# Transformer block on one core: normed rows stored from ScalarE's queue, tokens reordered within a block, h tiles rotated

## The chip, the cores and the metric

The kernel runs on one core of a Trainium2 chip. The time is that of one execution on the device, in microseconds (us). Before the change it is 1671.27 us, the median of 3 runs (1671.19 to 1672.89). All profile views come from one profiled execution.

A core has five engines that run side by side, each in the order of its own instructions: TensorE (PE, the matmuls; its weight loads are shown as PEld), VectorE (DVE), ScalarE (ACT), GpSimd (POOL) and SyncE (SP). SyncE issues most of the transfers. Transfers themselves are carried by 16 DMA engines. In a view, `SPq` and `ACTq` stand for the queue side of SyncE and ScalarE, `L903` for line 903 of the kernel.

## The reference

One block of a transformer over 2048 tokens of 1024 channels, in float32: attention with one head of 256 channels, then a feed-forward layer of 2752 hidden channels. Each half is a layer norm, the layer, another layer norm, and the residual.

```python
q, k, v = split(layernorm(x) @ Wqkv + bqkv)            # 2048 x 256 each
a  = softmax(q @ k.T / 16) @ v @ Wo + bo
x1 = x + layernorm(a)
xn = layernorm(x1)
h  = silu(xn @ W_gate.T) * (xn @ W_up.T)               # 2048 x 2752
out = x1 + layernorm(h @ W_down.T)
```

(This is the reference with its reshapes left out. The norms have no learned scale.)

## The kernel before

**Precision.** Each float32 operand of a matmul is split into a high part (a cast by ScalarE, L111) and a low part (a subtraction by VectorE, L112). Three matmuls of 128x128 weights against 128x512 then make one product (`mm3`, `mmc`, L867). The splits are most of what VectorE and ScalarE do.

**Stages.** (1) Up to about 200 us: q, k and v. (2) To about 480 us: the attention loop, 16 steps `i` of 128 query tokens, a "block". Step `i` turns the softmaxed scores of block `i` (`turn`), forms the scores of block `i + 1` (`scores`, `softmax`), multiplies by v (`attend`) and projects block `i - 1` (`turn_o`, L478, and `proj`). (3) To about 890 us: `gate_up` for the first 1024 tokens (`s = 0`), ten pairs of hidden blocks at about 40 us each. (4) To about 1042 us: `run_down` for the same tokens, which ends with `finish` for eight blocks. (5) To about 1440 us: `gate_up` for the other 1024 tokens (`s = 1`). (6) `run_down` for these, and the end.

**The feed-forward layer as seven products.** Both `gate_up` and `run_down` treat their matrices as 2 x 2 blocks and form seven products in place of eight. `gate_up` makes seven h matrices per pair (A11, A12, A22, S1, S2, S3, S4), each 128x512, in eight tiles `tmp[0..7]` under the names g11, u11, g12, u12, g22, u22 and g21 (the eighth is not used). Each is stored to DRAM (`put`, L898) and read back by `run_down`. The first products of a pair are copied from PSUM into g11 and u11 (the copy into u11 is L903). The last four stores of a pair are S1 from u22, S3 from u12, S2 from u11 and S4 from g12.

**From rows to columns.** The norm before the feed-forward layer gives rows (a token per partition), while the products want columns (a channel per partition). For a block `t`, `residual` forms x1, stores it to `x1_d[t]`, and leaves the normed rows in a tile `a` (L510, ScalarE). `regroup` stores these rows to `xn_d[t]` in a different order (L597, on SyncE) and reads the result back into tile `b` (L598, on SyncE, once L597 has landed). `xpose` transposes `b` in 32x32 squares on VectorE (L602, output with a stride of 4 elements) and stores the columns to `xT_d` (L604, SyncE). Blocks 0 to 7 (`EARLY = 8`) take this path in steps 2 to 10 of the attention loop: `residual` and `regroup` in step `t + 2`, `xpose` one step later. Blocks 8 to 15 take it during `gate_up` for `s = 0`, one block a pair. There the jobs of a pair (`jobs`) are called at fixed points between its products: the first does nothing, the second (`ahead`) transposes the block of the pair before and loads the next into `f4[2]` and `f4[3]`, the third (`behind`) calls `residual` and `regroup`.

**The end of a block.** `finish` normalises `y`, adds x1 and stores the block to `out` in two halves of 256 KB (L1105; the last block of all in one half and two quarters). For `s = 0` it reads x1 at L1094 into one of two ring tiles, `wr[1]` and `bo_s` (`raws2`), writes the result there or into `y` (L1104), stores it, and frees the tile. For `s = 1` the eight x1 tiles are loaded by L1343 once the room of the columns is free; the halves of that stage's stores alternate between SyncE and ScalarE.

**Order.** Each engine runs its instructions in a fixed order, which a list scheduler works out ahead of time from estimated durations; instructions given to `pin` keep the order in which the program names them. Waits between engines are semaphores. A tile is written again only when its last reader is done, a store's landing included.

Of the kernel before, what the change touches and what calls it, by code (L numbers as in the profile page):

```python
# [34 lines left out]
def block_kernel(ctx, tc, x, xt, wqk, wqk_t, wv, bqk, bv, wo, bo, wgu, wlast, wd, out):  # L35
# [556 lines left out]
        pin(nc.vector.tensor_tensor(wo_s[:, d, 1, :], wr[d], f32(wo_s[:, d, 0, :]), ALU.subtract))  # L592


    def regroup(t, a, b):

        nc.sync.dma_start(xn_d[t].rearrange("(i s) (g c) -> i s g c", i=4, g=4).rearrange("i s g c -> (s g) i c"), a.rearrange("p (i c) -> p i c", i=4))  # L597
        nc.sync.dma_start(b, xn_d[t])  # L598

    def xpose(t, a, b):  # L600

        nc.vector.transpose(a.rearrange("p (j s g) -> p g j s", j=8, g=4), b.rearrange("p (g j c) -> p g j c", g=4, j=8))  # L602
        d = xT_d[t // TB][:, (t % TB) * P : (t % TB + 1) * P]
        nc.sync.dma_start(d.rearrange("(j p) t -> p j t", p=P), a.rearrange("p (j t) -> p j t", j=8))  # L604

    def two(t):
        return t.rearrange("p (j n) -> p j n", j=2)
# [278 lines left out]
    def gate_up(s, p, wg, wu, bg, jobs, behind=None):  # L886


        ag, au, cg, cu = bg
        g11, u11, g12, u12, g22, u22, g21 = tmp[0:7]  # L890
        job = list(jobs)

        def background():
            if job:
                job.pop(0)()

        def put(name, t):
            nc.sync.dma_start(hd[s][p][name], t)  # L898

        prod(ag, wg, "A11", "B11")  # L900
        nc.scalar.copy(g11, ag)
        prod(au, wu, "A11", "B11")
        nc.scalar.copy(u11, au)  # L903
        background()
        prod(cg, wg, "A12", "B21")
        wg.slot[0].done()
        add(g11, cg, g11)
        silu(g11, g11)
        prod(cu, wu, "A12", "B21")
        wu.slot[0].done()  # L910
        add(u11, cu, u11)
        add(g11, g11, u11, ALU.mult)
        put("A11", g11)
        background()
        prod(ag, wg, "S2", "T2", False, behind and behind[0])
        nc.scalar.copy(g12, ag)
        with tc.issue_after(behind[1]) if behind else nullcontext():
            prod(au, wu, "S2", "T2", False)
        nc.scalar.copy(u12, au)
        with tc.issue_after(behind[1]) if behind else nullcontext():  # L920
            prod(cg, wg, "S1", "T1")
        wg.slot[1].done()
        with tc.issue_after(behind[1]) if behind else nullcontext():
            prod(cu, wu, "S1", "T1")
        wu.slot[1].done()
        background()
        prod(ag, wg, "S3", "T3", False)
        nc.scalar.copy(g22, ag)  # L928
        add(g22, cg, g22)
        silu(g22, g22)  # L930
        prod(au, wu, "S3", "T3", False)
        nc.scalar.copy(u22, au)
        add(u22, cu, u22)
        add(g22, g22, u22, ALU.mult)
        put("A22", g22)
        background()
        prod(ag, wg, "A22", "T4", False)
        wg.slot[3].done()
        silu(g21, ag)
        prod(au, wu, "A22", "T4", False)  # L940
        wu.slot[3].done()
        add(g21, au, g21, ALU.mult)
        put("A12", g21)
        prod(cg, wg, "S4", "B22", False)
        wg.slot[2].done()
        add(g12, cg, g12)
        silu(g12, g12)
        prod(cu, wu, "S4", "B22", False)
        wu.slot[2].done()
        add(u12, cu, u12)  # L950
        add(g12, g12, u12, ALU.mult)
        add(u22, g12, g22)
        add(u12, g11, g12, ALU.subtract)
        add(u11, u22, g11, ALU.subtract)
        add(g12, g21, u11, ALU.subtract)
        put("S1", u22)
        put("S3", u12)
        put("S2", u11)
        put("S4", g12)
# [126 lines left out]
    def finish(t, s, yt, spare=None, kept=False, parted=False):  # L1086


        if parted:
            st_, s = s, s[:, 12:32]  # L1090
            nc.vector.bn_aggr(s[:, 12:14], st_[:, 0:24])
        xt_ = raws2.get() if spare is None else spare
        if spare is None:
            nc.sync.dma_start(xt_, x1_d[t])  # L1094
        if not parted:
            nc.vector.bn_aggr(s[:, 12:14], s[:, 0:12])
        nc.vector.tensor_scalar(s[:, 14:15], s[:, 13:14], EPS, None, ALU.add)
        nc.gpsimd.tensor_tensor(s[:, 15:16], s[:, 14:15], mhalf, ALU.pow)
        nc.vector.tensor_scalar(s[:, 16:17], s[:, 12:13], -1.0, None, ALU.mult)
        nc.scalar.activation(yt[:, R], yt[:, R], AF.Identity, bias=s[:, 16:17])  # L1100
        nc.vector.tensor_scalar(yt[:, L], yt[:, L], s[:, 12:13], None, ALU.subtract)
        o = yt if kept else xt_
        for i, h in enumerate((L, slice(512, 768), slice(768, 1024)) if parted else (L, R)):
            nc.vector.scalar_tensor_tensor(o[:, h], yt[:, h], s[:, 15:16], xt_[:, h], ALU.mult, ALU.add)  # L1104
            (nc.sync if spare is None or i % 2 == 0 else nc.scalar).dma_start(out[t * P : (t + 1) * P, h], o[:, h])  # L1105
        if spare is None:
            raws2.free(xt_)

# [93 lines left out]
    for i in range(NT):  # L1202
        more = i + 1 < NT
        if i % TB == 0 and TB <= i < NT - TB:
            q_load(i // TB + 1)
        turn(i, 0)
        turn(i, 1)
        if i == NT - 1:
            for f in order[:2]:
                f.use()  # L1210
            for f, r in zip(order[4:6], f4[2:4]):
                f.load(r)
        if more:
            scores(i + 1, 0)
            scores(i + 1, 1)
        turn(i, 2)
        turn(i, 3)
        if more:
            scores(i + 1, 2)
            scores(i + 1, 3)  # L1220
            softmax(i + 1)

        if i < 2:
            wo_split(i)
        if i == 1:
            q_load(1)
        if i == 2:
            q_split(1, pin)
        if i % TB == 0 and TB <= i < NT - TB:
            q_split(i // TB + 1, pin)  # L1230
        if 2 <= i < EARLY + 2:
            residual(i - 2, *pair[(i - 2) % 3], sts[i - 2], pin)
            regroup(i - 2, *pair[(i - 2) % 3])
        if i < 3:
            nc.sync.dma_start(pair[i][1], x[i * P : (i + 1) * P, :])
        if i == NT - 1:
            for f in order[2:5]:
                f.use()
            for f, r in zip(order[6:8], (wr[1], f4[1])):
                f.load(r)  # L1240
        if i > 0:
            turn_o(i - 1)
        attend(i)
        if i > 0:
            proj(i - 1)
        if 3 <= i < EARLY + 3:
            xpose(i - 3, *pair[i % 3])
        if 3 <= i < EARLY:
            nc.sync.dma_start(pair[i % 3][1], x[i * P : (i + 1) * P, :])
        if 0 < i <= EARLY:  # L1250
            sts[i - 1] = out_stats(i - 1, pair[(i - 1) % 3][0])
        cb = i - EARLY - 3
        if 0 <= cb < 4:
            first_sums(cb, *room[cb % 2])
        if 0 <= cb + 1 < 4:
            first_load(cb + 1, *room[(cb + 1) % 2])
        if i == NT - 4:
            feed.pump()
        if i == NT - 2:
            for n in range(2):  # L1260
                slots.free(flat(a2[:, 2 * n : 2 * n + 2, :, :]))
            feed.pump()
            order = [t2[0], t13[0], t13[1], t13[2], t2[1], t13[3]] + t4
            spare = f4[2], f4[3], wr[1], xe
            for f, r in zip(order, spare):
                f.load(r)
# [17 lines left out]
    def late(p):  # L1284
        return EARLY + p - 1 if 1 <= p <= NT - EARLY else None

    def ahead(p):
        if p == 0:
            with tc.issue_after(last_o[0].ins):
# [3 lines left out]
                        order[9].load(f4[3])  # L1293
            return
        if late(p - 1):
            xpose(late(p - 1), *f4[2:4])
        if late(p):
            nc.sync.dma_start(f4[2], at_d[late(p)])
            nc.sync.dma_start(f4[3], x[late(p) * P : (late(p) + 1) * P, :])
        down_weights(p - 1)  # L1300

    def behind(p):
# [5 lines left out]
        with tc.issue_after(pairs[1][0].loading.ins) if p == 0 else nullcontext():  # L1308
            load_down(p)
        if late(p):  # L1310
            residual(late(p), *f4[2:4])
            regroup(late(p), *f4[2:4])

    for s in range(2):
        pairs, rest, dn = half[s]
        bg, other = (X, Y) if s == 0 else (Y, X)
        for p in range(NPAIR):
            jobs = [] if s else [lambda: None, lambda: ahead(p), lambda: behind(p)]
            if s == 0 and p == 0:
                jobs = [lambda: None, lambda: ahead(0), lambda: behind(0)]  # L1320
            if s == 0 and p == NPAIR - 1:
                jobs.append(lambda: down_weights(NPAIR - 1))
            gate_up(s, p, *pairs[p], bg, jobs, (turned.ins, projected.ins) if s == 0 and p == 0 else None)
# [15 lines left out]
        else:  # L1339
            xpool.release()  # L1340
            x1pool = pool("x1", side="right")
            x1 = [tl(x1pool, [P, C], F32, f"x1_{k}") for k in range(2 * TB)]
            run_down(s, dn, other, bg, x1, [lambda k=k: nc.sync.dma_start(x1[k], x1_d[2 * TB + k]) for k in range(2 * TB)])  # L1343
    xipool.release()
    wpool.release()
    v_pool.release()
# [40 lines left out]
```

## Time and profile before

| what | value |
|---|---|
| median of 3 runs | 1671.27 us |
| the profiled execution | 1671.44 us |
| its span, first to last instruction | 1669.7 us |
| granted TensorE clock, mean | 0.997 |
| DMA moved | 300.38 MB, mean 180 GB/s |

Where the transfers that the change touches stand (median time from issue to landing):

| transfer | issued by | count, size | us to landing |
|---|---|---|---|
| x1 stored, `x_d<-f` | SyncE | 14 x 512 KB | 2.6 |
| normed rows stored, `xn_d<-f` | SyncE | 14 x 512 KB | 3.7 |
| normed rows read, `f<-xn_d` | SyncE | 14 x 512 KB | 5.1 |
| x1 read, first half, `wr<-x_d` and `bo_s<-x_d` | SyncE | 4 + 4 x 512 KB | 5.2 and 4.5 |
| x1 read, second half, `x<-x_d` | SyncE | 8 x 512 KB | 7.8 |
| out stored, `out<-x` | SyncE, ScalarE | 8 + 7 x 256 KB | 2.1 and 2.0 |

The span is the time from the first to the last instruction of the profiled execution; the remaining 1.7 us of its time lie outside. In the views that follow, a line of a timeline gives the start, the length, the engine, the line of the kernel, the operation, the output and inputs by the program's names, the number of instructions merged into the line, and in brackets how long the engine had been idle before it and what it waited for. The chain of waits is followed back from the last instruction: each piece is what released the one after it. `x_d` in these names is `x1_d` of the code; `p_s` and `xi` hold the h tiles.

### The profile page before, as it was taken

How to read it: one execution, taken by the hardware profiler on the slowest of the kernel's cores; microseconds unless marked ns; L12 is line 12 of the kernel's file. 1: busy time of each engine (PE TensorE's matmuls, PEld its weight loads, DVE VectorE, ACT ScalarE, POOL GpSimd, SP SyncE). 2: the span in 40 equal slices, each digit the busy share in tenths (PEclk: the TensorE clock that was granted, in tenths of full speed). 3: DMA queues.
4: the chain of work that ended last, by engine and by line, in shares of the span. 5: the costliest groups of instructions: out<-in, count | busy, mean ns of one | idle time of the engine just before them, and what ended most of it. 6: DMA issues, size and time to landing. Idle time of an engine off the chain costs nothing.

```text
span 1669.7 us, 20815 instructions
## 1 busy us (share of the span) xinstructions
PE 1640.0 (98%) x7576; PEld 1361.9 (82%) x7576; DVE 1133.6 (68%) x1676; ACT 718.5 (43%) x1061; POOL 110.5 (7%) x157
## 2 busy tenths in 40 slices
PE   9999999999999999999999999999999999999998
PEld 8888888788887787877888888788888888888887
DVE  6656778778777777777588457965555665465458
ACT  5663545436443333433365444433333333354342
POOL 3120010000011111111000001100000000000001
PEclk9999999999999999999999999999999999999999
DMA  8451245555656666666568656533222223676653
GB/s 316 166 183 58 66 162 164 180 179 207 228 173 225 226 231 231 226 234 221 192 224 273 196 184 222 191 117 127 104 95 95 96 95 126 222 264 192 201 183 123
DMA packets 148183, 300.38 MB, mean 180 GB/s; under 512 B 14576, under 2 KB 39792, under 8 KB 148080
## 3 DMA queue, kind: packets, MB, share of 16 engines
q1 hardware_dynamic: 146928, 297.08, 52.6%
q10 hardware_dynamic: 1152, 1.97, 0.3%
q8 instruction: 59, 0.97, 0.2%
q14 instruction: 44, 0.36, 0.1%
HBM read 206.70 MB, written 92.29 MB: 179 GB/s over the span
## 4 chain that ended last, share of the span: by engine, by line
PE 73%; DVE 11%; DMA 9%; issue 3%; ACT 1%; POOL 1%; SPq 1%; DVEq 0%; POOLq 0%; ACTq 0%
PE bank L867 56%; PE bank L128 3%; PE bank L130 3%; PE bank L129 3%; DVE a L112 2%; DMA f<-xn_d 2%; PE bank L468 2%; DMA td_T<-f 2%; DVE p_s L881 2%; PE bank L246 1%; DVE small L118 1%; DVE wvo L112 1%; PE bank L452 1%; PE bank L469 1%; DVE f L602 1%
## 5 line engine op out<-in xcount | busy, mean ns | idle before, releaser
L867 PE MATMUL bank<-a 128*128 128x512 f32 (+1 forms) x960 | 226.4, 386 | 0.0
L867 PE MATMUL bank<-xb,a 128*128 128x512 f32 x912 | 212.4, 389 | 1.3 <-DVE a L112 1.3
L867 PEld LDWEIGHTS bank<-a 128*128 128x128 f32 x960 | 179.0, 188 | 36.6
L867 PEld LDWEIGHTS bank<-xb,a 128*128 128x128 f32 x912 | 170.9, 188 | 37.0 <-DVE a L112 1.7
L111 ACT CAST a<-f2p 128x1024 fp32r<-128x1024 f32 (+2 forms) x123 | 107.0, 870 | 127.9 <-PE bank L867 87.8
L112 DVE TENSOR_TENSOR a<-f2p,a 128x1024 fp32r<-128x1024 f32 (+2 forms) x123 | 122.4, 995 | 47.1 <-ACT a L111 43.1
L867 PE MATMUL bank<-kx,a 128*128 128x512 f32 x612 | 147.7, 390 | 0.0
L867 PEld LDWEIGHTS bank<-kx,a 128*128 128x128 f32 x612 | 115.3, 188 | 24.1
L112 DVE TENSOR_TENSOR a<-f,a 128x1024 fp32r<-128x1024 f32 (+1 forms) x70 | 79.9, 1142 | 61.6 <-ACT a L111 59.5
L867 PE MATMUL bank<-wvo 128*128 128x512 f32 (+1 forms) x498 | 120.9, 386 | 0.0
L881 DVE TENSOR_TENSOR p_s<-bank,p_s 128x512 f32<-128x512 f32 x96 | 65.1, 681 | 79.7 <-ACT p_s L903 52.0
L867 PEld LDWEIGHTS bank<-wvo 128*128 128x128 f32 x498 | 92.9, 188 | 18.9
L867 PE MATMUL bank<-kx,wvo 128*128 128x512 f32 x420 | 100.1, 389 | 0.0
L867 PE MATMUL bank<-a,a 128*128 128x512 f32 x420 | 99.6, 389 | 0.3 <-ACT xi L928 0.3
L111 ACT CAST a<-f 128x1024 fp32r<-128x1024 f32 (+1 forms) x70 | 57.5, 822 | 90.2 <-PE bank L867 88.8
L867 PEld LDWEIGHTS bank<-a,a 128*128 128x128 f32 x420 | 78.7, 188 | 17.1 <-ACT xi L928 0.7
L867 PEld LDWEIGHTS bank<-kx,wvo 128*128 128x128 f32 x420 | 78.8, 188 | 16.4
L112 DVE TENSOR_TENSOR wvo<-f,wvo 128x1024 fp32r<-128x1024 f32 (+1 forms) x47 | 54.7, 1163 | 50.9 <-ACT wvo L111 50.9
L867 PE MATMUL bank<-a1b,wvo 128*128 128x512 f32 x360 | 87.2, 390 | 1.5 <-DVE xi L881 1.4
L867 PEld LDWEIGHTS bank<-a1b,wvo 128*128 128x128 f32 x360 | 67.3, 188 | 16.8 <-DVE xi L881 2.8
L867 PE MATMUL bank<-kx 128*128 128x512 f32 (+1 forms) x339 | 78.5, 387 | 0.0
L867 PEld LDWEIGHTS bank<-kx 128*128 128x128 f32 x339 | 63.4, 188 | 13.0
(326 smaller groups left out, 3067.9 us busy)
## 6 DMA issues: line engine op xcount, KB each, us to landing
f2p<-wgu SPq DMA_DIRECT2D x41, 512.0 KB, 5.1
hd_S<-p_s SPq DMA_DIRECT2D x60, 256.0 KB, 4.8
f<-x SPq DMA_DIRECT2D x28, 512.0 KB, 5.6
f<-wgu SPq DMA_DIRECT2D x22, 512.0 KB, 3.5
wr<-wgu SPq DMA_DIRECT2D x21, 512.0 KB, 5.2
f<-wd SPq DMA_DIRECT2D x20, 512.0 KB, 4.2
hd_A<-xi SPq DMA_DIRECT2D x40, 256.0 KB, 2.0
td_T<-f SPq DMA_DIRECT2D x40, 256.0 KB, 4.9
```

The source lines that it names most:

```text
L111: nc.scalar.copy(hi, src)
L112: (lo_engine or nc.vector).tensor_tensor(lo, src, f32(hi), ALU.subtract)
L118: b = nc.vector.bn_stats(s[:, 6 * i : 6 * i + 6], h)
L128: pin(nc.tensor.matmul(o, w[0], m[0], start=first, stop=False))
L129: pin(nc.tensor.matmul(o, w[0], m[1], start=False, stop=False))
L130: return pin(nc.tensor.matmul(o, w[1], m[0], start=False, stop=last))
L246: pin(nc.tensor.matmul(b, xg[:, c, 0, cols], wv_s[:, c, :, :].rearrange("p a f -> p (a f)"), start=(c == 0), stop=False))
L452: nc.tensor.transpose(b[:, n * P : (n + 1) * P], p_s[:, k * P : (k + 1) * P], ident)
L468: nc.tensor.matmul(b, p[:, k, 0, :], vt(k).rearrange("p h d -> p (h d)"), start=(k == 0), stop=False)
L469: nc.tensor.matmul(b[:, D:], p[:, k, 1, :], vt(k, 0), start=False, stop=(k == NKB - 1))
L867: one = nc.tensor.matmul(o, w[i], m[j], start=first and n == 0, stop=last and n == 2, skip_group_check=chained)
L881: nc.vector.tensor_tensor(o, a, b, op)
```

## The change

- `regroup` becomes two functions. `spread` stores the normed rows from ScalarE's queue. `gather` reads them back on SyncE: in the attention loop at the start of the next step, in `gate_up` as the first job of the next pair (`between`).
- `xpose` writes its tile with contiguous output, and the transpose is pinned on VectorE. With it the tokens of a block come out in another order: token `4 s + g` of a block stands at place `32 g + s`.
- To undo that order, x1 is read and `out` is written through `turned_rows`: on the DRAM side 4 groups of 32 rows, with a stride of four rows within a group. It applies to the 8 reads of L1094, the 8 of L1343, and all 33 stores of L1105. The store of x1 keeps its order.
- The names of the h tiles rotate from pair to pair: the next g11 takes the unused tile, the next u11 the tile that held g22.
- `rooms`: in `gate_up` the two tiles of a late block, `f4[2]` and `f4[3]`, swap roles from pair to pair.

```diff
-    def regroup(t, a, b):
-
-        nc.sync.dma_start(xn_d[t].rearrange("(i s) (g c) -> i s g c", i=4, g=4).rearrange("i s g c -> (s g) i c"), a.rearrange("p (i c) -> p i c", i=4))
+    def spread(t, a):
+
+        nc.scalar.dma_start(xn_d[t].rearrange("(i s) (g c) -> i s g c", i=4, g=4).rearrange("i s g c -> (s g) i c"), a.rearrange("p (i c) -> p i c", i=4))
+
+    def gather(t, b):
         nc.sync.dma_start(b, xn_d[t])
 
     def xpose(t, a, b):
 
-        nc.vector.transpose(a.rearrange("p (j s g) -> p g j s", j=8, g=4), b.rearrange("p (g j c) -> p g j c", g=4, j=8))
+        pin(nc.vector.transpose(a.rearrange("p (j g s) -> p j g s", j=8, g=4), b.rearrange("p (g j c) -> p j g c", g=4, j=8)))
...
+    def turned_rows(d):
+        return d.rearrange("(s g) c -> g s c", g=4)
...
         g11, u11, g12, u12, g22, u22, g21 = tmp[0:7]
+        tmp[:] = [tmp[7], g22, g11, g21, u22, u12, u11, g12]
...
-            nc.sync.dma_start(xt_, x1_d[t])
+            nc.sync.dma_start(xt_, turned_rows(x1_d[t]))
...
-            (nc.sync if spare is None or i % 2 == 0 else nc.scalar).dma_start(out[t * P : (t + 1) * P, h], o[:, h])
+            (nc.sync if spare is None or i % 2 == 0 else nc.scalar).dma_start(turned_rows(out[t * P : (t + 1) * P, h]), o[:, h])
...
+        if 3 <= i < EARLY + 3:
+            gather(i - 3, pair[i % 3][1])
...
-            regroup(i - 2, *pair[(i - 2) % 3])
+            spread(i - 2, pair[(i - 2) % 3][0])
...
+    def rooms(p):
+        return f4[2 + p % 2], f4[3 - p % 2]
+
...
         if late(p - 1):
-            xpose(late(p - 1), *f4[2:4])
+            a, b = rooms(p - 1)
+            xpose(late(p - 1), a, b)
         if late(p):
-            nc.sync.dma_start(f4[2], at_d[late(p)])
-            nc.sync.dma_start(f4[3], x[late(p) * P : (late(p) + 1) * P, :])
+            a, b = rooms(p)
+            nc.sync.dma_start(a, at_d[late(p)])
+            nc.sync.dma_start(b, x[late(p) * P : (late(p) + 1) * P, :])
...
         if late(p):
-            residual(late(p), *f4[2:4])
-            regroup(late(p), *f4[2:4])
+            a, b = rooms(p)
+            residual(late(p), a, b)
+            spread(late(p), a)
+
+    def between(p):
+        if late(p - 1):
+            gather(late(p - 1), rooms(p - 1)[1])
...
-            jobs = [] if s else [lambda: None, lambda: ahead(p), lambda: behind(p)]
-            if s == 0 and p == 0:
-                jobs = [lambda: None, lambda: ahead(0), lambda: behind(0)]
+            jobs = [] if s else [lambda: between(p), lambda: ahead(p), lambda: behind(p)]
...
-            run_down(s, dn, other, bg, x1, [lambda k=k: nc.sync.dma_start(x1[k], x1_d[2 * TB + k]) for k in range(2 * TB)])
+            run_down(s, dn, other, bg, x1, [lambda k=k: nc.sync.dma_start(x1[k], turned_rows(x1_d[2 * TB + k])) for k in range(2 * TB)])
```

## The prediction

> **What bounds the kernel now.** I read the page's shares first, then TensorE's timeline for its waits, then the chain of waits and SyncE's timeline at the three places where the edited transfers stand.
>
> ```profile
> PE 1640.0 (98%) x7576; PEld 1361.9 (82%) x7576; DVE 1133.6 (68%) x1676; ACT 718.5 (43%) x1061; POOL 110.5 (7%) x157
> q1 hardware_dynamic: 146928, 297.08, 52.6%
> ```
>
> TensorE is the bound: 1640.0 of 1669.7 us. Only about 30 us are idle, so no edit off TensorE can win more than these plus lost clock, while any edit that starves it adds in full. The queue's line prices a DMA engine: 297.08 MB / (0.526 x 16 x 1669.7 us) = 21.1 GB/s. Where are the idle microseconds that the change can reach? TensorE's timeline, 500 to 800, with the windows around its longest wait (columns: stretch, length, busy of PE, PEld, DVE, ACT, POOL, clock, DMA share, GB/s):
>
> ```profile
> 533.60 1.66 PE L867 MATMUL bank<-qa,a 128*128 128x512 f32 x6 [2.23 <-ACT p_s L903]
> 574.15 1.65 PE L867 MATMUL bank<-qa,a 128*128 128x512 f32 x6 [2.17 <-ACT p_s L903]
> 655.96 2.93 PE L867 MATMUL bank<-qa,a 128*128 128x512 f32 x6 [3.01 <-ACT p_s L903]
> ```
>
> ```profile
> 650.00:660.00 10.00, 6.99 (x24) 5.27 (x23) 3.02 (x6) 1.70 (x3) 0.00 (x0) 0.76 0.94 319
> 660.00:670.00 10.00, 10.00 (x41) 8.19 (x40) 8.59 (x10) 3.53 (x5) 0.00 (x0) 0.90 0.72 230
> 670.00:680.00 10.00, 10.00 (x46) 8.26 (x44) 8.71 (x16) 4.71 (x8) 2.45 (x3) 1.00 0.49 170
> ```
>
> Once a pair TensorE waits for L903, the copy into u11. ACT in turn waits there, up to 5.43 us, for hd_S<-p_s: the store of the last pair's S2 still reads that tile. Six waits sum to 11.5 us. The longest costs more than itself: the clock falls to 0.76, and 650 to 670 holds 65 matmuls where two full windows hold 92; 27 fewer at 0.217 us are 5.9, of which 3.0 is the wait and 2.9 the clock.
>
> Next, the chain of waits where the first half's rows are finished, and the end of the kernel:
>
> ```profile
> 1026.81 4.53 DMA out<-wr
> 1031.41 3.79 DMA wr<-x_d
> 1036.06 0.76 DVE wr L1104
> 1037.26 4.46 DMA bo_s<-x_d
> ...
> 1046.83 1.41 DVE f L1104 x2
> 1048.23 1.15 DVE a L112
> 1049.42 461.79 PE bank L867 x2036
> ```
>
> ```profile
> 1644.61 22.52 SPq L1105 DMA_DIRECT2D out<-x  x9
> ```
>
> Before 1049 the set of output stores, then x1 reloads, through two ring tiles (wr, bo_s) is itself on the chain; behind it TensorE runs unbroken for 462 us. The last nine SyncE stores leave from 1644.61 on, while TensorE works until 1662.9.
>
> **Part 1: the h tiles rotate.** u11 takes the tile that held g22, whose store A22 left in the middle of the last pair. This removes the 11.5 us on L903 and, at the one deep wait, 2.9 of clock: -14.4 at best. The next wait behind is DVE's xi L881 and ACT's xi L928 (0.92, 0.47, 0.30); these 1.7 us stay. I take -14.
>
> **Part 2: stores of normed rows to ACT's queue, reload a step later.** 16 stores leave SyncE at 0.38 us of issue each (526.09, L597), 6 us in sum, and the 16 reloads no longer make it wait for a landing (xn_d<-f: 3.7 us). ACT takes 16 issues at the 0.34 us its own stores show, 5.4 us; each stands right behind L510, an ACT instruction, so it waits only for its engine's own result; behind it stand the L111 casts and u11's copy, 0.34 us late. ACT is 43% busy and idle 1.68 to 5.43 us at a time there: nothing on the path. Without that cover it is 0.34 x 8 = 2.7 us in gate_up. The reload keeps its place on SyncE, after the puts of S1, S3, S2 and S4, and now finds its rows landed; what DVE waits before L602 (19.4 us in 10) mostly goes, on an engine that is not the bound.
>
> **Part 3: the pinned transposes.** The strided L602 takes 2.03 us, 16 times. With contiguous output none is shown: below, the 1.21 us of a 128x1024 tensor_tensor (L506); above, 2.03. In attention it now has a fixed place, behind L491 and ahead of the next L118, L265, L440, L441 and L481. DVE is idle there 1.13 and 1.63 us a step (before L112 at 238.90 and L491 at 250.80), so at most 2.03 - 1.1, about 1 us, reaches TensorE: +8 over 8 steps. Against it TensorE's waits of that stretch, 4.6 (200 to 300) and 1.3, can go: -5.9. The value nearest to both ends is 0, range -5.9 to +8. In gate_up DVE has room (229 of 300 us busy).
>
> **Part 4: reordered rows.** So that the transposes can write contiguously, tokens change places inside a block, and every read of x1_d and store to out now has a DRAM pattern of 4 x 32 rows, row stride 16 KB, where all DMAs of before begin with a count of 64 or 128. 16 reads of 512 KB and 33 stores (31 of 256 KB, 2 of 128) do this. No row shows such a pattern. From below: as today. A 256 KB out<-x lands in 2.0 us and a 512 KB x_d<-f in 2.6, so 256 KB more on 16 engines cost 0.6 us, and about 1.3 is fixed. Above: the transfer is shared by its outermost count, 4 engines of 16, and its engine time is four times as long: 512 KB / (4 x 21.1 GB/s) = 6.2 us, or by the difference of the two landings, 4 x 2 x 0.6 = 4.8. I take T = 5.5 per 512 KB (half for 256), the upper end: equal shares of 4 are what the pattern offers, and no row has a smaller count to show otherwise.
>
> The Trainium skill, "DMA: Bandwidth & Descriptors", states this rule (its rules for kernel authors, and how many engines a transfer uses): an outermost dimension below 16 confines the whole DMA to that many engines. By it the sum is the slower one below, without it the faster one; the trace has no row on either side, and the page speaks against the change.
>
> What T does, place by place:
> - *Finishing the first half.* From 1025.63 to the last x1 reload SyncE issues 12 half stores and 6 reloads, 12 T, and 4 ordinary 512 KB loads at 1.5, each behind the other on the same engines, with wr and bo_s handed from store to reload. 1025.6 + 66 + 6 + 1.3 = 1098.9, where L1104 used it at 1066.57: +32.3. TensorE had some 2.5 us of slack (ACT L919 at 1069.16, needed at 1072.2): +30. DVE works in order, so the stall holds the splits (L112) behind it and TensorE. T = 4.8: +21; 6.2: +38.
> - *The eight x1 loads of the second half.* Issued from 1440.52, 8 T = 44; behind them on SyncE and the engines stand run_down's weights (L848, L849), wanted for the eighth step at 1472.97 (steps are 12 matmuls, 2.72 us, the first at 1453.9). Two 256 KB loads 1.5, landing 1.3, split 2.5: 1440.5 + 49.3 = 1489.8, some 1491 with the small stores between: +18. T = 4.8: +12; 6.2: +24.
> - *The tail.* 8 blocks of out, 8 T, from 1644.6: 1688.6 + 1.3, and about 1 of issue, 1691 against 1669.7: +21. T = 4.8: +16; 6.2: +27.
> - Stalls this long lower the clock as at 650 (2.9 us for one): +4 for the lot, 3 to 5.
>
> **Sum.** Own time 1671.44 (span 1669.7 and 1.7 around it; the median is 1671.27, within 0.2). -14 + 0 + 30 + 18 + 21 + 4 = +59: 1730. With T = 4.8 and the attention gain 1671 - 14 - 6 + 21 + 12 + 16 + 3 = 1703; with T = 6.2 and its loss 1671 - 14 + 8 + 38 + 24 + 27 + 5 = 1759.
>
> **Rivals.** (A) The turned transfers spread as today's do. Then only parts 1 to 3 count: 1671 - 14, 1657, from 1651 to 1665. For it: same bytes, same 4 KB rows. Against: 4 outer entries. (B) The same, and a new wait eats the gain: the pinned transpose costs its +8 and u11's wait only moves, to the spare tile that g11 now takes or to SyncE's later puts, giving back 4 to 7 of the 14: 1668 to 1672, no change. For it: SyncE issues those puts only at 526 to 530, just ahead of the copy. (C) Slower without part 4: the transposes hold DVE in order whenever their reload is late. They do so above 0.9 us a transpose (16 x 0.9 = 14): at the 1.9 us that DVE waits for f<-xn_d today (19.4 / 10), 16 x 1.9 - 14 = +16, 1687. Against it: the reload no longer follows its store.
>
> **Chances.** Forecast 0.82, A 0.12, B 0.04, C 0.02. Range 1690 to 1760: the forecast's bounds, 1703 and 1759, let down most of the way to C, as the low T rests on two landings alone; A and B, 0.16, are left out. What can be told from no change is about 0.2%, 3.3 us: faster 0.12 (A), within it 0.04 (B), slower 0.84.
>
> **What would show it.** Right: x_d reads landing in 7 us or more alone and 256 KB stores in 4 or more; DVE idle before the finishing of rows by DMA; TensorE waits in 1045 to 1100 and near 1475; stores ending some 20 us after TensorE; no waits on u11's copy. Wrong: reads of x1 landing in 4 to 5 us as now (then A); DVE idle before the transposes of 1 us or more (C); a contiguous transpose above 2.03 us, or TensorE waits at L478 that stay (part 3).

## The result, and the profile after

The changed kernel takes 1738.57 us (median of 4 runs, 1736.52 to 1740.45), the kernel before 1671.23 (4 runs). The ratio is 1.0401, 95% interval 1.0383 to 1.0419: 67 us slower. The profiled execution has a span of 1736.3 us.

The first two lines of the page of the changed kernel, engines and the first queue:

```profile
PE 1652.9 (95%) x7576; PEld 1370.7 (79%) x7576; DVE 1122.6 (65%) x1676; ACT 717.9 (41%) x1061; POOL 108.4 (6%) x157
...
q1 hardware_dynamic: 137988, 288.69, 50.1%
```

The bytes are the same, so are the instruction counts of every engine, and VectorE and ScalarE are busy a little less. (Lines stand up to six further down in this kernel: L872 is L867 of the kernel before, L853 is L848, L1110 is L1104 and L1111 is L1105.) TensorE's idle time grew from 30 to 83 us, and its own work is longer by 13 us, with a mean granted clock of 0.974 in place of 0.997. Where? Both kernels issue the same 7576 matmuls, in an order that differs, by the operands' names, in 588 places, most of them between 200 and 320 us. So I set the start of the n-th matmul in the one profile against that in the other. The shift between them changes by more than 0.3 us at these places only (us, negative is earlier; attention is taken to end at 417 us of the kernel before, where its last matmul stands, not at 480):

| stretch | changed against before |
|---|---|
| attention | -6.7 |
| `gate_up`, first half | -18.1 |
| `run_down`, first half, at the first two x1 reads | +7.1 |
| finishing the first half | +40.1 |
| the eight x1 loads of the second half | +22.4 |
| behind TensorE's last matmul | +22.0 |
| sum, with -0.2 ahead of attention (spans 1736.3 and 1669.7) | +66.6 |

Lost time stands at the reordered transfers. The chain of waits of the changed kernel at two of these places (start, length, what):

```profile
1008.86 9.10 DMA out<-wr
1018.03 10.58 DMA wr<-x_d
1029.48 0.76 DVE wr L1110
1030.25 8.46 DMA out<-wr
1038.77 10.32 DMA wr<-x_d
...
1055.25 15.88 DMA wr<-x_d
...
1081.09 11.78 DMA wr<-wgu
...
1487.10 9.17 SPq L853
1496.32 17.25 DMA f2p<-hd_A
```

Before, the same steps were 4.53 for out<-wr and 3.79 for wr<-x_d. The loads of weights and of h that stand behind them (wr<-wgu, f2p<-hd_A) are late with them. TensorE's timeline says the same; its longest wait at each place:

```profile
889.59 0.79 PE L872 MATMUL bank<-a 128*128 128x512 f32 x1 [3.10 <-ACT a L111]
...
1036.95 1.22 PE L872 MATMUL bank<-xb,a 128*128 128x512 f32 x2 [9.04 <-ACT a L111]
...
1502.44 0.79 PE L872 MATMUL bank<-wvo 128*128 128x512 f32 x1 [15.30 <-ACT wvo L111]
```

The releaser named is ScalarE's cast, but the cast had itself waited for a load; at 1036.95 it did so by way of VectorE, which had stood 14.41 us at L1110 for wr<-x_d. The clearest view is the end. SyncE's stores, and the windows behind TensorE's last matmul (columns as in the prediction: the last three are the clock, the share of the 16 DMA engines and GB/s):

```profile
1689.16 30.48 SPq L1111 DMA_DIRECT2D out<-x  x9
```

```profile
1710.00:1720.00 10.00, 0.00 (x0) 0.00 (x0) 2.93 (x8) 0.72 (x1) 0.78 (x1) 0.58 0.26 102
1720.00:1735.00 15.00, 0.00 (x0) 0.00 (x0) 0.00 (x0) 0.00 (x0) 0.00 (x0) 0.50 0.25 94
```

No engine computes any more, only stores run, and they keep 0.25 of the DMA engines' time busy, what 4 of 16 give. At 94 to 102 GB/s a full 512 KB takes 5.1 to 5.6 us.

### The profile page after: what moved, and what is told of

It is laid out like the page before. It is cut to its first block, busy times and chain, and to the rows that moved or that the text cites. A ratio compares the mean times of both kernels' runs of the same rounds, so it can differ in the third digit from the quotient of the medians.

```text
span 1736.3 us, 20865 instructions
## 1 busy us (share of the span) xinstructions
PE 1652.9 (95%) x7576; PEld 1370.7 (79%) x7576; DVE 1122.6 (65%) x1676; ACT 717.9 (41%) x1061; POOL 108.4 (6%) x157
## 4 chain that ended last, share of the span: by engine, by line
PE 77%; DMA 9%; DVE 6%; SPq 2%; issue 2%; ACT 1%; POOL 1%; ACTq 0%; DVEq 0%; POOLq 0%
PE bank L872 56%; PE bank L128 4%; PE bank L130 4%; PE bank L129 4%; PE bank L468 3%; DMA wr<-x_d 2%; DVE a L112 2%; PE bank L469 1%; PE bank L452 1%; DMA xn_d<-f 1%; PE bank L246 1%; DMA out<-wr 1%; SPq L1359 1%; DMA f2p<-hd_S 1%; DMA f2p<-hd_A 1%
## 5 line engine op out<-in xcount | busy, mean ns | idle before, releaser
L872 PE MATMUL bank<-a 128*128 128x512 f32 (+1 forms) x960 | 229.7, 390 | 3.6 <-ACT a L111 3.1
L872 PE MATMUL bank<-xb,a 128*128 128x512 f32 x912 | 217.6, 396 | 15.3 <-ACT a L111 9.0
L872 PEld LDWEIGHTS bank<-xb,a 128*128 128x128 f32 x912 | 173.9, 191 | 53.2 <-ACT a L111 9.5
L872 PEld LDWEIGHTS bank<-a 128*128 128x128 f32 x960 | 180.5, 189 | 41.9 <-ACT a L111 3.5
L872 PE MATMUL bank<-kx,a 128*128 128x512 f32 x612 | 145.1, 389 | 0.0
L872 PE MATMUL bank<-wvo 128*128 128x512 f32 (+1 forms) x498 | 123.1, 391 | 16.0 <-ACT wvo L111 15.3
L872 PEld LDWEIGHTS bank<-kx,a 128*128 128x128 f32 x612 | 115.0, 188 | 24.0
L872 PEld LDWEIGHTS bank<-wvo 128*128 128x128 f32 x498 | 94.3, 191 | 36.2 <-ACT wvo L111 15.7
L872 PE MATMUL bank<-kx,wvo 128*128 128x512 f32 x420 | 101.4, 394 | 0.0
L872 PE MATMUL bank<-a,a 128*128 128x512 f32 x420 | 99.7, 390 | 0.6 <-ACT p_s L934 0.6
L872 PEld LDWEIGHTS bank<-kx,wvo 128*128 128x128 f32 x420 | 80.1, 191 | 16.9
L872 PE MATMUL bank<-a1b,wvo 128*128 128x512 f32 x360 | 88.1, 394 | 5.1 <-DVE xi L886 5.1
L872 PEld LDWEIGHTS bank<-a,a 128*128 128x128 f32 x420 | 78.7, 188 | 17.6 <-ACT p_s L934 1.0
L886 DVE TENSOR_TENSOR xi<-bank,xi 128x512 f32<-128x512 f32 (+1 forms) x90 | 61.0, 682 | 47.4 <-PE bank L872 40.5
L872 PEld LDWEIGHTS bank<-a1b,wvo 128*128 128x128 f32 x360 | 68.7, 191 | 19.9 <-DVE xi L886 5.6
L872 PE MATMUL bank<-kx 128*128 128x512 f32 (+1 forms) x339 | 80.7, 394 | 2.0 <-ACT kx L111 1.2
L886 DVE TENSOR_TENSOR p_s<-bank,p_s 128x512 f32<-128x512 f32 x80 | 53.9, 682 | 43.8 <-PE bank L872 39.9
```

The source lines that it names most:

```text
L872: one = nc.tensor.matmul(o, w[i], m[j], start=first and n == 0, stop=last and n == 2, skip_group_check=chained)
L886: nc.vector.tensor_tensor(o, a, b, op)
```

## The experiments

**What makes the reordered transfers slow.** Three causes fit so far: the outermost count (4), the row stride (16 KB), or a fixed cost of the pattern. Four kernels tell them apart; beside them the kernel before took 1672.37 us.

`plain_rows` takes the reordering out:

```diff
     def turned_rows(d):
-        return d.rearrange("(s g) c -> g s c", g=4)
+        return d
```

> The changed kernel with x1 read and out written without the reordering (so x1 is added to the wrong tokens of a block, and out stands in the reordered order). If all that was lost lies in the reordered transfers, as the prediction says, only its parts 1 to 3 are left: by TensorE's shifts between the two profiles 6.9 us gained in attention and 18.1 in gate_up, so 1671 - 25 = 1646, 1643 to 1650. If something else of the change costs too (pinned transposes, ScalarE's stores, a new order on SyncE), some of the 67 us stay: above 1655.

Measured: 1646.76 us, ratio 0.9854 (0.9839 to 0.9869). All four losses are gone (0.0, +0.2, 0.0, 0.0 in the order of the table), attention keeps -6.8 and `gate_up` -15.3. Everything that was lost lies in the reordered transfers. It is lost in two ways, as TensorE's idle time and as its clock. This is its line here, for the same matmuls as in the changed kernel:

```profile
PE 1634.6 (99%) x7576; PEld 1360.6 (83%) x7576; DVE 1120.6 (68%) x1676; ACT 717.0 (44%) x1061; POOL 110.2 (7%) x157
```

Against it TensorE's own work in the changed kernel is 18.3 us longer (1652.9), at a mean granted clock of 0.974 in place of 0.999, and its idle time 70.4 us longer (83.4 and 13.0). `gate_up` gains 2.8 less than in the changed kernel, in two waits of 0.72 and 1.29 us for the copy into g22 and in clock. The order of instructions on each engine there, by line and tile, is the same in both. The profiled execution is the longest of its four (1649.42, the others 1645.74 to 1647.53), so 2.8 us may be this one execution's; in the profiles of `groups_2` and `groups_16`, with the same order, `gate_up` gains 13.7 and 17.4. A difference of 3 or 4 us in `gate_up` between two profiles means little.

`groups_2` and `groups_16` change the count, `g=4` to `g=2` and `g=16`, and with it the row stride, to 8 and 64 KB.

> The changed kernel with 2 groups of 64 rows (row stride 8 KB) in place of 4 of 32 (16 KB) in every read of x1 and store of out; the order of tokens is then not the right one. By the outermost count: 2 engines, T doubles from 5.5 to about 11 us per 512 KB; 12 T in the finishing of the first half, 8 T at the x1 loads, 8 T in the tail, some 2 T at the first two reads: +30 x 5.5 = +165, about 1900, 1850 to 1950. By the row stride (rows far apart are slow): a smaller stride, so no more than 1739. By a fixed cost of the less simple pattern: the same as 4 groups, 1739.

Measured: 1887.02 us, one run. The same end in its windows:

```profile
1840.00:1860.00 20.00, 0.00 (x0) 0.00 (x0) 4.34 (x11) 1.44 (x2) 0.78 (x1) 0.50 0.13 51
```

0.13 is the share of 2 engines of 16, and the bytes per second are half. Place by place the loss grows from 7.1, 40.1, 22.4 and 22.0 us to 13.6, 100.5, 60.9 and 61.2. With 12, 8 and 8 times T on the path of the last three, doubling T added 60.4 / 12, 38.5 / 8 and 39.2 / 8: by this growth T on 4 engines is 4.8 to 5.0 us, a little under the 5.1 to 5.6 of the rates above.

> The same with 16 groups of 8 rows (row stride 64 KB). By the outermost count: 16 engines again, as fast as without the reordering, 1646, 1643 to 1652, with SyncE's issue still at 0.5 us. By the row stride: 1739 or more. By a fixed cost of the pattern: 1739.

Measured: 1648.01 us, one run, with rows 64 KB apart; no loss at any place but 0.8 at the end. Stride and a fixed cost are out.

`four_dmas` keeps the very rows and addresses of the changed kernel:

```diff
+    def by_groups(queue, sbuf, dram, store):
+        d = turned_rows(dram)
+        for g in range(4):
+            rows = sbuf[32 * g : 32 * g + 32]
+            queue.dma_start(d[g], rows) if store else queue.dma_start(rows, d[g])
...
-            nc.sync.dma_start(xt_, turned_rows(x1_d[t]))
+            by_groups(nc.sync, xt_, x1_d[t], False)
...
```

The stores of `out` and the eight x1 loads change in the same way.

> The changed kernel, with each reordered transfer made of four, one for each group of 32 rows: the same rows, addresses and strides as in the changed kernel, but an outermost count of 32 each. By the outermost count: full speed of the transfers, 1646, and above it only what four times as many issues cost: about 72 issues of 0.4 us, 29 us of SyncE, in the 40 us of finishing the first half, and up to 2 us at the last store; 1646 to 1665. By the row stride: still 1739 or more.

Measured: 1650.44 us, ratio 0.9877 (0.9861 to 0.9894). The finishing of the first half costs +0.1, in spite of four times the issues; only the end pays, +3.8, where issues stand behind the last results (SyncE issues 36 stores in 25.07 us, ScalarE's last eight take 4.50 us). With its transfers cut this way the change is 22 us faster than the kernel before.

`plain_second_reads` takes the reordering from one place, the eight x1 loads of the second half:

```diff
-            run_down(s, dn, other, bg, x1, [lambda k=k: nc.sync.dma_start(x1[k], turned_rows(x1_d[2 * TB + k])) for k in range(2 * TB)])
+            run_down(s, dn, other, bg, x1, [lambda k=k: nc.sync.dma_start(x1[k], x1_d[2 * TB + k]) for k in range(2 * TB)])
```

> The changed kernel with the eight x1 loads of the second half (one of the places of part 4) read plainly, so that x1 of these rows is added to the wrong tokens; all other reordered transfers stay. If each place costs by itself what TensorE's shift shows there, 22.4 us go and the rest stays: 1738.6 - 22.4 = 1716, 1713 to 1720. If the places share one cost (the same late work, met again further on), the later place takes part of it over: 1725 or more.

Measured: 1718.56 us, one run; that place costs 0.0, the others 9.7, 41.0 and 22.0. The other places cost 2.6 us more at most than in the changed kernel: what this place cost was its own and was not met again further on.

**Where the gain comes from.** The prediction puts -14 on the rotation, nothing on the moved stores and nothing on attention. Four kernels, beside 1671.83 us before.

`rotate_only` is the kernel before with one line more:

```diff
         g11, u11, g12, u12, g22, u22, g21 = tmp[0:7]
+        tmp[:] = [tmp[7], g22, g11, g21, u22, u12, u11, g12]
```

> The kernel before, with only the rotation of the h tiles. As the prediction has it, u11's copy waits no more for the store of S2: 11.5 us of waits and 2.9 of clock go, all in gate_up, and nothing in attention: 1671 - 14 = 1657, 1654 to 1660. If the 18 us that gate_up gained in the changed kernel came from the moved stores of normed rows (SyncE issues the puts sooner), the rotation alone is worth under 7: above 1664.

Measured: 1673.63 us, ratio 1.0010 (1.0001 to 1.0020). Nothing is gained. The waits on u11's copy did go. Their place was taken by waits for the copy into g22 (L929), 10.6 us in 7, where u11's had been 11.5 in 6; one pair in its timelines:

```profile
661.88 2.02 DVE L602 STREAM_TRANSPOSE f<-f 128x1024 f32<-128x1024 f32 x1 [6.75 <-DMA f<-xn_d]
...
669.22 0.62 ACT L111 CAST a<-f2p 128x512 fp32r<-128x512 f32 x1 [4.95 <-DVE f2p L790]
669.75 0.58 ACT L929 COPY xi<-bank 128x512 f32<-128x512 f32 x1
```

```profile
670.38 5.74 PE L867 MATMUL bank<-a,a 128*128 128x512 f32 x24 [1.58 <-ACT xi L929]
676.99 3.28 PE L867 MATMUL bank<-a1b,wvo 128*128 128x512 f32 x13 [0.87 <-DVE xi L881]
```

Read from the top: VectorE stands 6.75 us before the transpose, because the normed rows are not back. Behind the transpose, in order, comes the weights' sum L790; ScalarE's cast waits for it; behind the cast, in order, stands the copy into g22 (L929), ready long before; and TensorE waits for that copy. In the kernel before, TensorE had already stood 0.8 to 3.0 us at u11's copy by then in six pairs, and waits on the copy into g22 were all but absent (0.30). I read the two as alternatives: removing the first bought the second. `later_xpose` below tests the second.

`spread_only` is the other half: stores of normed rows on ScalarE's queue, reload a step later, transposes strided and not pinned, no rotation.

> The kernel before with only the store of normed rows on ScalarE's queue, the reload a step later and the two tiles that swap roles; transposes strided and not pinned, tokens in their order, no rotation. By the prediction's part 2 nothing on the path: 1671, 1667 to 1673, with the waits on u11's copy still there. If the moved stores are what attention gained (6.9 us): 1664. If they also free the puts of S2: 1650 to 1660.

Measured: 1659.38 us, ratio 0.9927 (0.9908 to 0.9946); attention -0.8, `gate_up` -11.2. The part that was costed at nothing brings most of the gain. Why? SyncE's waits in the kernel before (what waited, for what; us in total, times, longest), and its puts at one pair there; after them the same pair of this kernel (whose L903 is the put, L898 before; u11's copy is L908 here):

```profile
SPq L597 <- ACT f L510: 41.9, 14, 6.3
```

```profile
648.25 0.38 SPq L597 DMA_DIRECT2D xn_d<-f  x1
648.73 0.45 SPq L898 DMA_DIRECT2D hd_S<-xi  x1
649.27 2.08 SPq L898 DMA_DIRECT2D hd_S<-p_s  x2
```

```profile
640.38 0.42 ACTq L597 DMA_DIRECT2D xn_d<-f  x1
640.39 0.87 SPq L903 DMA_DIRECT2D hd_S<-p_s  x2
```

Before, the store L597 stood on SyncE ahead of the puts and waited there for ScalarE's L510, and the puts, whose data were ready, waited with it. Set against the copy into g11 (ScalarE, 648.8 and 640.9), S2's put left at +1.4 us before and leaves at -0.1 now. Set against one and the same matmul of each pair, u11's copy starts 1.2 us sooner (8.8 us after it in place of 9.9, means of seven pairs, which lie between 5.0 sooner and 1.3 later), and TensorE's waits there fall from 11.5 us in 6 to 4.3 in 5. The wait that the prediction read as one on a tile was in part one on a queue. In part only: ScalarE still waits for the store of S2 at u11's copy, 50.0 us in 17 where it was 47.5 in 17, but in four of these seven pairs it ends earlier against TensorE's work. The run also moves the reload and swaps the two tiles; what each is worth was not told apart.

`strided_pinned` has both, with natural token order:

```diff
-        pin(nc.vector.transpose(a.rearrange("p (j g s) -> p j g s", j=8, g=4), b.rearrange("p (g j c) -> p j g c", g=4, j=8)))
+        pin(nc.vector.transpose(a.rearrange("p (j s g) -> p g j s", j=8, g=4), b.rearrange("p (g j c) -> p g j c", g=4, j=8)))
...
     def turned_rows(d):
-        return d.rearrange("(s g) c -> g s c", g=4)
+        return d
```

> The changed kernel with the transpose's strided output back, still pinned in the same place, so that tokens keep their order and x1 and out are read and written plainly. The transpose takes 2.03 us again in place of 1.24. If attention's 6.9 us came from the place (behind the o sum and the projection's first half) the rest stays: 1647 to 1650. If they came from the 0.8 us saved in each of eight steps: 1653, with waits for L471 or L481 back.

Measured: 1658.71 us, ratio 0.9917 (0.9900 to 0.9934); attention -3.2, `gate_up` -7.9. Against `plain_rows` it loses 3.6 in attention and 7.4 in `gate_up`, for 0.78 us in each of 16 transposes: in `gate_up` 0.9 us of TensorE for each transpose (the medians of their runs differ by 12.0 in all). So the contiguous output is worth half of what it saves on VectorE in attention and all of it in `gate_up`, as if VectorE were on the path there, not off it. In `gate_up` it waits 53.8 us in 8 transposes for their reload, as here:

```profile
652.29 2.02 DVE L604 STREAM_TRANSPOSE f<-f 128x1024 f32<-128x1024 f32 x1 [7.84 <-DMA f<-xn_d]
```

Of attention's 6.8 us in `plain_rows`, 0.8 came with the moved stores (`spread_only`), 2.4 more with the place, and 3.6 with the length. With the place came another order of TensorE's matmuls in some 380 places between 200 and 320 us, the same in `plain_rows` and `strided_pinned`; the two were not told apart.

`group_norm_store` has the contiguous transposes and natural order, by storing the normed rows in four transfers:

```diff
-        nc.scalar.dma_start(xn_d[t].rearrange("(i s) (g c) -> i s g c", i=4, g=4).rearrange("i s g c -> (s g) i c"), a.rearrange("p (i c) -> p i c", i=4))
+        for g in range(4):
+            d = xn_d[t][:, 256 * g : 256 * g + 256].rearrange("(i s) c -> s i c", i=4)
+            nc.scalar.dma_start(d, a[32 * g : 32 * g + 32].rearrange("p (i c) -> p i c", i=4))
...
     def turned_rows(d):
-        return d.rearrange("(s g) c -> g s c", g=4)
+        return d
```

> The changed kernel with contiguous transposes, but with tokens in their order: the normed rows are stored by four transfers of 32 rows each on ScalarE's queue, so that each group of 32 tokens lands where the contiguous transpose needs it, and x1 and out are read and written plainly. 48 more issues on ScalarE at 0.37 us, 18 us in sum, beside work on an engine busy for 41%: as without the reordering, 1647, 1643 to 1651. If ScalarE's issues reach the path (each sits ahead of casts that TensorE wants), up to 1665.

Measured: 1667.23 us, ratio 0.9969 (0.9957 to 0.9982): the upper case. Four issues take 4.05 us of ScalarE, not 4 x 0.37, and TensorE waits behind them:

```profile
246.22 4.05 ACTq L599 DMA_DIRECT2D xn_d<-f  x4
...
250.36 0.59 ACT L111 CAST a<-bank 128x512 fp32r<-128x512 f32 x1 [3.62 <-DMA xn_d<-f]
...
251.00 0.49 PE L468 MATMUL bank<-a,a 128*128 128x512 f32 x1 [2.59 <-ACT a L111]
```

Attention comes out at +2.6 where `plain_rows` has -6.8, and `gate_up` at -8.0. Why an issue of 32 rows in pieces of 1 KB takes a microsecond was not followed up.

**A transpose in the right place.** If VectorE waits in order for a reload, the transpose must move behind the weights' sums. `later_xpose` does this to `strided_pinned`:

```diff
     def ahead(p):
...
-        if late(p - 1):
-            a, b = rooms(p - 1)
-            xpose(late(p - 1), a, b)
-        if late(p):
-            a, b = rooms(p)
-            nc.sync.dma_start(a, at_d[late(p)])
-            nc.sync.dma_start(b, x[late(p) * P : (late(p) + 1) * P, :])
         down_weights(p - 1)
 
     def behind(p):
...
-        if late(p):
-            a, b = rooms(p)
-            residual(late(p), a, b)
-            spread(late(p), a)
+        if late(p - 1):
+            a, b = rooms(p - 1)
+            xpose(late(p - 1), a, b)
+        if late(p):
+            a, b = rooms(p)
+            nc.sync.dma_start(a, at_d[late(p)])
+            nc.sync.dma_start(b, x[late(p) * P : (late(p) + 1) * P, :])
+
+    def last(p):
+        if late(p):
+            a, b = rooms(p)
+            residual(late(p), a, b)
+            spread(late(p), a)
+        if p == NPAIR - 1:
+            down_weights(p)
...
-            jobs = [] if s else [lambda: between(p), lambda: ahead(p), lambda: behind(p)]
-            if s == 0 and p == NPAIR - 1:
-                jobs.append(lambda: down_weights(NPAIR - 1))
+            jobs = [] if s else [lambda: between(p), lambda: ahead(p), lambda: behind(p), lambda: last(p)]
```

> strided_pinned with one move in gate_up: the transpose of a late block, and the loads of the next that follow it, are called one job later (behind S1's products, with the weights' loads), and the norm and store of the next block in a fourth job. VectorE then forms the weights' sums of the next pair ahead of the transpose. If what TensorE waits for there is VectorE, held by a transpose whose reload is not there (7.8 us idle at 652.29 in strided_pinned, and the copy into g22 on ScalarE behind the late cast), gate_up's 7 remaining us go: 1658.7 - 7 = 1651, 1649 to 1653, with no TensorE waits on the copy into g22. If these waits come from the transpose's length alone, or from VectorE's load in all, they stay: 1658; if the late norm and store now end behind the next pair's start, 1660 or more.

Measured: 1647.95 us against 1671.67, ratio 0.9857 (0.9840 to 0.9873). `gate_up` gains 19.2 in place of 7.9, 11 us from an order alone; VectorE does not wait for a reload before any transpose, and TensorE shows no wait from 480 to 860. So the waits that `strided_pinned` has there, and most likely those of `rotate_only`, came from VectorE being held in order by the transposes. The next block's loads, norm and store moved in the same run, so their share is not told apart.

`later_no_rotation` then takes the rotation out of it.

```diff
-        tmp[:] = [tmp[7], g22, g11, g21, u22, u12, u11, g12]
```

> later_xpose without the rotation of the h tiles, so that u11's copy again writes the tile whose store of S2 may still be on its way. Rotation alone gained nothing. If that was because the late transposes took the place of the wait on u11's copy, the rotation is worth something once they are moved: waits on u11's copy of 0.5 to 1.2 us in most pairs, as in spread_only (4.4 us in all), and 1648.0 + 4 to 6 = 1652 to 1654. If moving the stores of normed rows to ScalarE's queue has made the rotation needless, 1648.

Measured: 1648.43 us against 1670.82, ratio 0.9866 (0.9849 to 0.9882): the rotation is needless here. ScalarE still waits 26.6 us in 18 at u11's copy, 1.5 each, but TensorE never for it. Expected was a loss of 4 to 6, so this missed. No run showed a gain from the rotation; whether it pays with the stores back on SyncE and the transposes moved, or in the changed kernel itself, was not tried.

`mixed_later` joins what paid: contiguous transposes and four transfers for the blocks of the first half only, strided ones and plain rows for the second, `later_xpose`'s order.

```diff
+        if t < EARLY:
+            pin(nc.vector.transpose(a.rearrange("p (j g s) -> p j g s", j=8, g=4), b.rearrange("p (g j c) -> p j g c", g=4, j=8)))
+        else:
+            pin(nc.vector.transpose(a.rearrange("p (j s g) -> p g j s", j=8, g=4), b.rearrange("p (g j c) -> p g j c", g=4, j=8)))
...
+            if spare is None:
+                by_groups(nc.sync, o[:, h], out[t * P : (t + 1) * P, h], True)
+            else:
+                (nc.sync if i % 2 == 0 else nc.scalar).dma_start(out[t * P : (t + 1) * P, h], o[:, h])
...
```

> The whole change where it paid: contiguous transposes for blocks 0 to 7 (the attention loop), whose x1 reads and out stores go in four transfers of 32 rows; strided ones for blocks 8 to 15, so that their x1 reads, out stores and the tail stay as before; rotation and ScalarE's stores kept; the later transposes of later_xpose. Attention 6.9, gate_up 18 to 20, the tail 0 against four_dmas' 3: 1671.5 - 25 to 27 = 1645 to 1647. If the four transfers hold up the finishing of the first half or the moved jobs bring a new wait: 1650 or more.

Measured: 1646.33 us (1646.00 to 1646.67), ratio 0.9846 (0.9831 to 0.9860): faster than both kernels, by 25 us than the one before and 92 than the changed one. Attention -6.8, `gate_up` -18.9, finishing -0.1, the end +0.6.

## Why the prediction was right, and where it was not

The forecast was 1730, within 1690 to 1760; measured 1738.57. Its main mechanism, reordered transfers on four engines, holds, and so do the signs of its large terms. Where the gain comes from it had mostly wrong. Taken by its own steps:

- **Part 4, four engines: right, and shown.** The end of the kernel runs at a DMA share of 0.25 with count 4, 0.13 with 2, and with counts of 16 and 32 the three places inside the kernel lose 0.1 us at most. The Trainium skill's rule ("DMA: Bandwidth & Descriptors", on how many engines a transfer uses) is that an outermost count below 16 leaves a transfer at most that many engines; all four counts agree with it. T was taken as 5.5; the rates at the end give 5.1 to 5.6, the growth from 4 to 2 engines 4.8 to 5.0.
- **Finishing the first half: +30 forecast, +40.1 measured.** The mechanism holds. The last L1110 on a reloaded tile stands at 1085.04, where before's 1066.57, less the 17.9 already gained, would be 1048.7: +36.4, for +32.3 forecast. The steps take 8.5 to 15.9 us, with ordinary loads among them and SyncE up to 4.57 us at a single issue. The step that failed is the slack of 2.5 us: the next half's weights (wr<-wgu, 11.78 us) were late as well, and TensorE waited 5.13 and 1.86 us for their products after that.
- **The x1 loads: +18 forecast, +22.4 measured**, with the clock in it: 0.75 from 1480 to 1500, 0.66 in the next 10 us. **The tail: +21 forecast, +22.0 measured.**
- **The clock: +4 forecast, 3 to 5, about +18 measured.** TensorE's own work is 1652.9 us with the reordered transfers and 1634.6 without them (`plain_rows`). This is the term that was most mis-sized: it was carried over from one wait of 3 us, and these are waits of up to 15.3. The rest of the 88.7 us between the two spans, 70.4, is idle time, where the three places were put at 69. So the figures measured inside the kernel hold some clock, and less idle time than they seem to.
- **Missed: the first two reads of x1.** They were not among the places. Issued at 864.61 and 868.65, they have no user for 140 us, but two h loads issued behind them land late (f2p<-hd_S, 17.33 us), and TensorE waits: +7.1 with its clock. The step "12 half stores and 6 reloads" counted transfers by when their data are wanted, not by what queues behind them.
- **Part 1, -14 for the rotation: wrong in its cause.** `gate_up` gained 18.1, but the rotation alone gives +1.8 (ratio 1.0010). The wait moved, as rival B says, though to another place than B names: the copy into g22, by way of VectorE's transpose. What the rotation is worth inside the changed kernel was not measured.
- **Part 2, nothing on the path: wrong.** The moved stores alone gave -12.4. The prediction counted the issue times on SyncE, 6 us, but not that L597 waited there 41.9 us in 14 for L510, with the puts behind it. VectorE's waits before the transposes, which were to go for the most part, grew (see rival C).
- **Part 3: 0 forecast within -5.9 to +8; -6.7 measured in attention**, just outside. The contiguous transpose takes 1.24 us, next to the lower bound of 1.21. "In `gate_up` DVE has room" was wrong: 229 of 300 us busy is a share. Of the 68 us that VectorE is idle there in the changed kernel (500 to 800), 38.7 stand right in front of the transposes, with the weights' sums waiting behind.
- **Rival C** did not decide, but its mechanism is real, and its sign, VectorE idle 1 us or more before the transposes, is there. VectorE's waits, before and in the changed kernel:

```profile
DVE f L602 <- DMA f<-xn_d: 19.4, 10, 3.5
DVE f L604 <- DMA f<-xn_d: 42.8, 8, 7.0
```

In all, gains of 14 and losses of 73 were forecast, and gains of 24.8 and losses of 91.6 measured. Both were a good deal short, and that the errors of 11 and 19 us partly cancel is luck.

## What to carry to other kernels

Look at the outermost count of a transfer's pattern before its bytes: an access order that saves VectorE 0.8 us can put every load and store that undoes it on a quarter of the engines; the same rows in transfers with a count of 16 or 32 cost 0.8 and 3.9 us here, in place of 92. When a wait on a tile is read, ask what stands ahead of its releaser in the queue, and what the engine would meet next if the wait were gone; two waits in one stretch can be alternatives, and removing one of them then shows no gain. An instruction that waits for a reload belongs behind the work that its engine could do meanwhile.

## What the runs showed of the hardware

- Ordinary transfers issued behind a few on four engines land late: 512 KB of weights took 11.78 us, 256 KB of h 17.25.
- SyncE itself then stands at issuing: a single issue of L853 took 9.17 us and the issue of four x1 loads 13.80, where one takes 0.3 to 0.55 otherwise; what is behind it on SyncE waits too.
- The store of normed rows landed in 3.6 us on SyncE's queue (median of 16, kernel before) and in 5.8 on ScalarE's (`plain_rows`), up to 8.9 in `gate_up`: moved to the second queue, it let SyncE's transfers go ahead but landed later itself.
- Between long waits TensorE's granted clock did not come back in the changed kernel: 0.50 from 1040 to 1050, and 0.83 from 1070 to 1080, where it worked without a pause.
